# Cross-attention scores: the queries' scale moved into VectorE's pass over the scores, and the exponents' offset made by one fused pass

## The chip, the cores and the metric

The kernel runs on one core of a Trainium2 chip, as one launch. The metric is the device time of that launch in microseconds (us). The engines are TensorE (PE in the profile; PEld is its loading of weights), VectorE (DVE), ScalarE (ACT), GpSimd (POOL) and SyncE (SP), which only issues transfers.

## The reference, cut to what matters

The program is one block: a cross-attention of 512 query rows (4 x 128) to 8192 context rows, a causal self-attention, and a feed-forward network with 4-bit weights. The change lies in the cross-attention, which has 16 heads of 64 and quantises queries, keys, values and the attention weights:

```python
q = _fq_sym(q, axis=-1)          # integers -127..127, times one scale per query and head
k = _fq_sym(k, axis=-1)          # the same, one scale per key and head
v = _fq_sym(v, axis=2)
attn = jnp.einsum('bhqd,bhkd->bhqk', q, k)
attn = jax.nn.softmax(attn.astype(jnp.float32), axis=-1)
attn = _fq_unsigned(attn, axis=-1)      # rounded to multiples of (row maximum)/255
out = jnp.einsum('bhqk,bhkd->bhqd', attn, v)
```

A score is therefore (product of integers) x (scale of the key) x (scale of the query). Since the row maximum of a softmax maps to 255, the rounded weight is round(exp(score - maximum + log 255)), and the sum of the unrounded exponentials divides the result at the end.

## The kernel before, in words

The launch has stages in this order: the projection of the queries, the projection of the context to values and then to keys (up to about 1500 us), the cross-attention (about 1505 to 2144 us), the output projection and self-attention, and the feed-forward network. Only the cross-attention is touched.

Its work is cut into 64 **units** (L766), one for each head h and each block t of 128 query rows. A unit has 128 rows of scores against 8192 keys, in 8 steps of SC = 1024 keys. The loop at L981 runs over all 512 steps, and every engine's order is the order in which this loop emits instructions (a manual schedule, nothing is rearranged):

- `scores(n, g)` (L769): two matrix products (L782) put 128x1024 integer scores into PSUM (tile `sc`, two buffers). Then one custom VectorE pass, `tensor_tensor_reduce` (L789), multiplies them by the keys' scales (`sk`, spread over the partitions by GpSimd at L762), writes them to the tile `e` in SBUF, and takes the running maximum of the 1024 columns. The compiler makes two instructions of it: the pass, and a read of the accumulator into column g of `mx` (128x8).
- `maximum(n)` (L800), after the eighth step: a reduction of the eight maxima (L804) and a TENSOR_SCALAR (L806) which multiplies by minus the query's scale and adds log 255. The result `m` (128x1) is the offset of the exponents. Each of the two waits for the one before it.
- `exponentials(n, c)` (L812), twice per unit and one unit later: ScalarE forms exp(scale x e + m) over 4096 columns, rounds to int16 and sums the row (L817). The query's scale is this instruction's scale operand.
- `transposes` (L826) and `dma_transposes` (L843) turn the integers, half of them on TensorE with a copy by ScalarE (L839), half by a transfer; `values` (L874) multiplies them by the values (L881), and at the end of each head four short VectorE operations (L893 to L904) finish the result.

`sq` (L198) holds the queries' scales, 128 x 4 blocks x 16 heads. Ahead of the stage L744 makes `sqs` of it, once with the sign plus and once with minus, by two VectorE products. The tile `e` has three buffers of half a unit each, `mx` and `m` four.

The custom operation computes out = (in0 op0 in1) x scale and accumulates with op1, starting from `scalar`. Its `scale` may be a constant or a column with one value per partition.

Rows outside the stage that the prediction compares: L391 (shifts of the packed 4-bit weights, in one part by a constant, in another by the column `shifts`), L394 (a bit mask on 128x1024), L159 and L1427 (a tile times a constant plus a tile), L142 and L1167 (a layer norm's tile minus one column times another), L1534 (a 128x1 value times and plus constants), and L1541 (a tile times the column `ms` plus a tile).

Of the kernel before, what the change touches and what calls it, by code (L numbers as in the profile page):

```python
# [34 lines left out]
F32 = mybir.dt.float32  # L35
# [6 lines left out]
ALU = mybir.AluOpType  # L42
AX = mybir.AxisListType
# [3 lines left out]
P = 128  # L47
B, S, C = 4, 128, 1024
NT = B * S // P
NC = C // P  # L50
H, D = 16, 64
# [7 lines left out]
NSC = NK // SC  # L59
# [19 lines left out]
LOWEST = -3.0e38  # L79
# [7 lines left out]
def tile_perceiver(  # L87
# [26 lines left out]
    nc = tc.nc  # L114
# [83 lines left out]
    sq = qpool.tile([P, NT, H], F32, name="sq")  # L198
# [535 lines left out]
    with tc.tile_pool(name="at_e", bufs=1) as at_e, tc.tile_pool(  # L734
        name="at_s", bufs=4
    ) as small, tc.tile_pool(name="at", bufs=2) as at, tc.tile_pool(
        name="at_ps", bufs=3, space=PSUM
    ) as at_ps:
        sc_ps = sc_s.enter_context(tc.tile_pool(name="sc_ps", bufs=2, space=PSUM, side="right"))
        sv = small.tile([P, C], F32, name="sv", tag="sv", bufs=1)  # L740

        sqs = small.tile([P, 2, NT, H], F32, name="sqs", tag="sqs", bufs=1)
        for i in range(2):
            nc.vector.tensor_scalar_mul(sqs[:, i], sq, 1.0 - 2.0 * i)  # L744
        ident16 = small.tile([P, P], F16, name="ident16", tag="ident16", bufs=1)
        nc.scalar.copy(ident16, ident)
        vqs = {}
# [21 lines left out]
        def scores(n, g):  # L769

            h, t = units[n]
            if g == 0:
                mx = small.tile([P, NSC], F32, name="mx", tag="mx")
                state[n] = {"mx": mx, "e": [], "a": []}
            if g % (NSC // NEC) == 0:
                e = at_e.tile([P, EC], F32, name="e", tag="e", bufs=3)
                state[n]["e"].append(e)
            ps = sc_ps.tile([P, SC], F32, name="sc", tag="sc")

            for i in range(2):  # L780
                rows = slice(D * i, D * i + D)
                nc.tensor.matmul(  # L782
                    ps[:, ts(i, 512)],
                    lhsT=qT[rows, h, ts(t, P)],
                    rhs=kts[h, g // 2][rows, ts(g % 2, 512)],
                    start=True,
                    stop=True,
                )
            nc.vector.tensor_tensor_reduce(  # L789
                out=state[n]["e"][-1][:, ts(g % (NSC // NEC), SC)],  # L790
                in0=ps,
                in1=sks_at[h, g],
                scale=1.0,
                scalar=LOWEST,
                op0=ALU.mult,
                op1=ALU.max,
                accum_out=state[n]["mx"][:, g : g + 1],
            )

        def maximum(n):  # L800
            h, t = units[n]
            st = state[n]
            m = st["m"] = small.tile([P, 1], F32, name="m", tag="m")
            nc.vector.tensor_reduce(m, st["mx"], AX.X, ALU.max)  # L804

            nc.vector.tensor_scalar(  # L806
                m, m, sqs[:, 1, t, h : h + 1], math.log(255.0), ALU.mult, ALU.add
            )
            if t == 0:
                sums[h] = small.tile([P, NT, NEC], F32, name="sum", tag="sum")  # L810

        def exponentials(n, c):  # L812
            h, t = units[n]
            st = state[n]
            a = at.tile([P, EC], I16, name="a", tag="a", bufs=3)
            st["a"].append(a)
            nc.scalar.activation(  # L817
                a,
                st["e"][c],
                AF.Exp,  # L820
                bias=st["m"],
                scale=sqs[:, 0, t, h : h + 1],
                accum_out=sums[h][:, t, c : c + 1],
            )

# [154 lines left out]
        with tc.manual_schedule():  # L980
            for s in range(n_steps + LAG_V):  # L981
# [8 lines left out]
                if g % (NSC // NEC) == 0 and 1 <= n <= len(units):  # L990
                    exponentials(n - 1, g // (NSC // NEC))
                if n < len(units):
                    h, t = units[n]
                    scores(n, g)
                    if t == NT - 1 and h + 1 < H:

                        if g < NKC:
                            load_keys(h + 1, g)
                        spread_scales(h + 1, g)
                        if g == NSC - 1 and h + 2 < H:  # L1000
                            load_rows(h + 2)
                    if g == NSC - 1:
                        maximum(n)
# [306 lines left out]
    with tc.manual_schedule():  # L1310
# [10 lines left out]
        for h, (w, n) in enumerate(PARTS):  # L1321
# [13 lines left out]
            if h in (3, 5):  # L1335
                m = (h - 3) // 2
# [71 lines left out]
    with tc.tile_pool(name="ff_t", bufs=2) as ff_t, tc.tile_pool(  # L1408
        name="ff_a", bufs=1
# [36 lines left out]
        with tc.tile_pool(name="ff_g", bufs=2) as ff_g:  # L1446
# [13 lines left out]
            with tc.tile_pool(name="g_ps", bufs=2, space=PSUM) as g_ps, tc.tile_pool(  # L1460
                name="u_ps", bufs=2, space=PSUM
# [17 lines left out]
        with tc.tile_pool(name="ff_h", bufs=1) as ff_h, tc.tile_pool(  # L1479
            name="y_ps", bufs=1, space=PSUM  # L1480
# [135 lines left out]
```

## Time and profile before

| | us |
|---|---|
| median of 3 runs (2855.76 to 2858.63) | 2857.21 |
| the profiled execution | 2854.13 |
| its span, first to last instruction | 2852.4 |
| TensorE busy | 2652.6 |
| VectorE busy | 2421.2 |
| ScalarE busy | 1267.0 |
| GpSimd busy | 455.7 |

In the profile, a row of a group reads: line, engine, operation, output tile <- input tiles, shapes, the count, then after the bar the busy time of all in us and the mean of one in ns, and after the second bar the idle time of that engine just before these instructions, with what ended it. The page cuts the span into 40 slices, in which a digit is the busy share in tenths. A timeline row gives the start and the length in us; rows of one line in a run are merged, with their number behind the x. A table by windows gives for each stretch its length, the busy time of each engine with the number of instructions in brackets, the granted clock of TensorE, and the busy share and rate of the DMA engines. The mean granted TensorE clock of the profiled execution was 0.987.

### The profile page before, as it was taken

The numbers are of one execution on the slowest core, as the hardware profiler recorded it, in microseconds if no ns is written. First come the engines' busy times: TensorE is split into PE (matmuls) and PEld (weight loads), VectorE is DVE, ScalarE is ACT, GpSimd is POOL, SyncE is SP. The second block draws the span as 40 slices with busy tenths as digits, with TensorE's granted clock in tenths as the row PEclk, the third lists the DMA queues.
The fourth block names the chain that finished last, engine by engine and source line by source line (L and its number), as shares of the span: only waits on it lengthen the run. The fifth ranks groups of instructions, "written<-read, shape, count | busy, mean of one in ns | idle before, by whom it ended". The sixth has DMA issues, their size and how long they took to land.

```text
span 2852.4 us, 41096 instructions
## 1 busy us (share of the span) xinstructions
PE 2652.6 (93%) x15496; PEld 2059.5 (72%) x15496; DVE 2421.2 (85%) x3960; ACT 1267.0 (44%) x1404; POOL 455.7 (16%) x608
## 2 busy tenths in 40 slices
PE   8999999999999999999996777787778899999998
PEld 3788888888878888888884555555555777788886
DVE  6899999555699998888879999999997898876674
ACT  4211211112323333333217999999994244333332
POOL 0011111000012222222113332233312000000000
PEclk9999999999999999999998999999999999999999
DMA  5555565222447777777536888877875222122222
GB/s 188 170 200 201 194 212 207 104 96 95 146 106 198 192 192 186 188 186 191 130 88 144 164 167 165 154 149 161 164 145 153 76 83 67 52 96 96 94 92 96
DMA packets 450631, 412.66 MB, mean 145 GB/s; under 512 B 354872, under 2 KB 359544, under 8 KB 450432
## 3 DMA queue, kind: packets, MB, share of 16 engines
q1 hardware_dynamic: 402848, 251.70, 36.3%
q0 software_dynamic: 46528, 157.29, 17.2%
q8 instruction: 122, 2.00, 0.3%
q10 hardware_dynamic: 1056, 1.05, 0.2%
q14 instruction: 77, 0.63, 0.1%
HBM read 220.14 MB, written 104.34 MB: 114 GB/s over the span
## 4 chain that ended last, share of the span: by engine, by line
PE 70%; DVE 21%; issue 4%; POOL 2%; ACT 1%; DMA 1%; DVEq 0%; ACTq 0%
PE kv_a L342 32%; PE kv_b L342 16%; DVE e L789 14%; PE acc_a L1130 3%; PE up_a L165 3%; PE gate_a L165 3%; PE y_a L1503 3%; POOL sk L762 2%; PE q_ps L292 2%; PE acc_b L1130 1%; PE up_b L165 1%; PE gate_b L165 1%; PE y_b L1503 1%; PE a_pt L832 1%; DVE sw_l L158 1%
## 5 line engine op out<-in xcount | busy, mean ns | idle before, releaser
L342 PE MATMUL kv_b<-w_d,c_d 128*128 128x512 f32 x2048 | 806.0, 394 | 0.3 <-DVE c_d L159 0.3
L342 PE MATMUL kv_a<-w_h,c_h 128*128 128x512 f32 x2048 | 806.3, 394 | 0.0
L342 PE MATMUL kv_a<-w_l,c_l 128*128 128x512 f32 x2048 | 806.0, 394 | 0.2 <-ACT w_l L246 0.2
L789 DVE CUSTOM_DVE_ANT_0 e<-sc,sk 128x1024 f32<-128x1024 f32 x512 | 593.0, 1220 | 8.1 <-PE sc L782 7.0
L817 ACT ACTIVATE a<-e,m,sqs 128x4096 int16<-128x4096 f32 x128 | 486.9, 3804 | 24.1 <-DVE m L806 23.8
L342 PEld LDWEIGHTS kv_a<-w_l,c_l 128*128 128x128 f32 x2048 | 384.8, 188 | 89.6 <-ACT w_l L246 0.6
L342 PEld LDWEIGHTS kv_b<-w_d,c_d 128*128 128x128 f32 x2048 | 384.8, 188 | 89.5 <-DVE c_d L159 0.8
L342 PEld LDWEIGHTS kv_a<-w_h,c_h 128*128 128x128 f32 x2048 | 384.9, 188 | 88.8 <-issue 0.2
L155 ACT ACTIVATE c_h<-c_raw 128x1024 fp32r<-128x1024 f32 x128 | 135.2, 1057 | 418.9 <-PE kv_a L342 404.6
L356 DVE SCALAR_TENSOR_TENSOR f<-kv_a,bkv 128x512 f32<-128x512 f32 x256 | 175.8, 687 | 163.4 <-PE kv_a L342 162.8
L782 PE MATMUL sc<-kt,qT 64*128 64x512 bf16 x1024 | 205.5, 393 | 104.9 <-DVE mx L789 100.8
L581 ACT CAST kst<-kT 128x512 bf16<-128x512 int16 x128 | 89.4, 699 | 302.3 <-DMA kT<-ki 302.3
L832 PE MATMUL a_pt<-ident,a 128*128 128x128 f32 x1024 | 174.3, 295 | 21.1 <-ACT a L817 16.4
L357 DVE SCALAR_TENSOR_TENSOR f<-kv_b,f 128x512 f32<-128x512 f32 x256 | 176.7, 690 | 20.3 <-DVE f L356 0.9
L762 POOL PARTITION_BROADCAST sk<-sk_row x120 | 142.3, 1297 | 312.3 <-DVE mx L789 312.2
L832 PEld LDWEIGHTS a_pt<-ident,a 128*128 128x128 f32 x1024 | 111.4, 144 | 86.9 <-ACT a L817 48.9
L782 PEld LDWEIGHTS <-qT 64*128 64x128 bf16 x1024 | 75.3, 93 | 132.7 <-issue 102.7
L158 DVE TENSOR_TENSOR fw_l<-fw_raw,fw_h 128x1024 fp32r<-128x1024 f32 x64 | 78.3, 1224 | 99.4 <-ACT fw_h L155 99.3
L158 DVE TENSOR_TENSOR c_l<-c_raw,c_h 128x1024 fp32r<-128x1024 f32 x128 | 155.7, 1217 | 5.8 <-ACT c_h L155 5.6
L159 DVE SCALAR_TENSOR_TENSOR c_d<-c_l,c_raw 128x1024 fp32r<-128x1024 f32 x128 | 156.3, 1221 | 2.3
L155 ACT ACTIVATE fw_h<-fw_raw 128x1024 fp32r<-128x1024 f32 x64 | 67.8, 1060 | 175.4 <-PE y_a L1503 71.6
L548 ACT CAST vq<-vi 128x1024 f16<-128x1024 int16 x64 | 67.0, 1046 | 171.0 <-DVE vi L541 123.9
(211 smaller groups left out, 4104.9 us busy)
## 6 DMA issues: line engine op xcount, KB each, us to landing
c_raw<-in_ctxT SPq DMA_DIRECT2D x128, 512.0 KB, 3.6
v_d<-f POOLq DMA_DIRECT2D x64, 512.0 KB, 3.1
vl<-v_d POOLq DMA_DIRECT2D x64, 512.0 KB, 4.2
gu_d<-w_ffn POOLq DMA_DIRECT2D x44, 512.0 KB, 3.1
fw_raw<-gu_d SPq DMA_DIRECT2D x42, 512.0 KB, 3.2
k_d<-kst POOLq DMA_DIRECT2D x128, 128.0 KB, 3.5
vq_d<-vq POOLq DMA_DIRECT2D x32, 512.0 KB, 5.2
kt<-k_d SPq DMA_DIRECT2D x64, 256.0 KB, 3.5
```

The source lines that it names most:

```text
L155: nc.scalar.mul(hi, src, 1.0 - 0.5 / UP)
L158: nc.vector.tensor_tensor(lo, src, hi, ALU.subtract)
L159: nc.vector.scalar_tensor_tensor(df, lo, -1.0 - UP, src, ALU.mult, ALU.add)
L165: nc.tensor.matmul(ps, lhsT=lhs(i, k), rhs=rhs(i, k), start=(k == 0 and i != 1), stop=(k == NC - 1 and i != 0),)
L342: nc.tensor.matmul(ps, lhsT=tokens[s][i][:, k, :], rhs=w3[s < KT][k][i][:, ts(n, 512)], start=(k == 0 and i != 1), stop=(k == NC - 1 and i ...
L356: nc.vector.scalar_tensor_tensor(f, a, 1.0 + 1.0 / UP, bias[s < KT][n], ALU.mult, ALU.add)
L357: nc.vector.scalar_tensor_tensor(f, b, -1.0 / UP, f, ALU.mult, ALU.add)
L762: nc.gpsimd.partition_broadcast(tile_of_scales(h, g), sks_at[h][32 * c : 32 * c + 1, ts(half, SC)], channels=P)
L782: nc.tensor.matmul(ps[:, ts(i, 512)], lhsT=qT[rows, h, ts(t, P)], rhs=kts[h, g // 2][rows, ts(g % 2, 512)], start=True, stop=True,)
L789: nc.vector.tensor_tensor_reduce(out=state[n]["e"][-1][:, ts(g % (NSC // NEC), SC)], in0=ps, in1=sks_at[h, g], scale=1.0, scalar=LOWEST, o ...
L817: nc.scalar.activation(a, st["e"][c], AF.Exp, bias=st["m"], scale=sqs[:, 0, t, h : h + 1], accum_out=sums[h][:, t, c : c + 1],)
L832: nc.tensor.transpose(pt[:, i, :], a[:, at_word + P * i : at_word + P * i + P], ident)
```

## The change

The query's scale goes into the VectorE pass, whose scale operand becomes a column of `sq`. What it writes to `e` and what it takes the maximum of are then complete scores, so ScalarE's exponential has the constant 1.0 as scale. The offset log 255 - max is formed in one custom pass over the eight maxima: it adds -log 255 (a new constant tile `log255`, 128x8, written once by GpSimd), multiplies by -1, and takes the minimum. Like the large pass it is compiled to two instructions, the pass and a read of the accumulator. `sqs` and its two products go. The order of the instructions on each engine is otherwise the same.

```diff
-        sqs = small.tile([P, 2, NT, H], F32, name="sqs", tag="sqs", bufs=1)
-        for i in range(2):
-            nc.vector.tensor_scalar_mul(sqs[:, i], sq, 1.0 - 2.0 * i)
+        log255 = small.tile([P, NSC], F32, name="log255", tag="log255", bufs=1)
+        nc.gpsimd.memset(log255, -math.log(255.0))
...
                 in1=sks_at[h, g],
-                scale=1.0,
+                scale=sq[:, t, h : h + 1],
                 scalar=LOWEST,
...
             m = st["m"] = small.tile([P, 1], F32, name="m", tag="m")
-            nc.vector.tensor_reduce(m, st["mx"], AX.X, ALU.max)
-
-            nc.vector.tensor_scalar(
-                m, m, sqs[:, 1, t, h : h + 1], math.log(255.0), ALU.mult, ALU.add
+            nc.vector.tensor_tensor_reduce(
+                out=st["mx"],
+                in0=st["mx"],
+                in1=log255,
+                scale=-1.0,
+                scalar=-LOWEST,
+                op0=ALU.add,
+                op1=ALU.min,
+                accum_out=m,
             )
...
                 bias=st["m"],
-                scale=sqs[:, 0, t, h : h + 1],
+                scale=1.0,
                 accum_out=sums[h][:, t, c : c + 1],
```

## The prediction

> **What bounds the kernel now.** I read the page's slices first, to find the stage that the change lies in, then a table by windows of that stage, then its costliest groups, and at last the order of VectorE's instructions in time.
>
> The slices, 71.3 us each:
>
> ```profile
> PE   8999999999999999999996777787778899999998
> ...
> DVE  6899999555699998888879999999997898876674
> ACT  4211211112323333333217999999994244333332
> ```
>
> In the slices at 22 to 30 (1505 to 2144 us) TensorE drops to 7 or 8 tenths while VectorE and ScalarE stand at 9. This is the cross-attention, and all that the diff touches is in it. Is VectorE or ScalarE the bound there? The table by windows (length, then busy time of PE, PEld, DVE, ACT, POOL):
>
> ```profile
> 1550.00:1700.00 150.00, 117.03 (x1444) 82.24 (x1444) 147.93 (x289) 144.82 (x123) 41.30 (x47) 0.99 0.81 162
> 1700.00:1850.00 150.00, 117.51 (x1455) 82.53 (x1454) 147.91 (x289) 145.88 (x123) 46.77 (x54) 0.99 0.82 160
> ```
>
> VectorE works 148 of 150 us, ScalarE 145, TensorE 117. VectorE is the bound, with ScalarE 2% behind it. The groups say who waits for whom:
>
> ```profile
> L789 DVE CUSTOM_DVE_ANT_0 e<-sc,sk 128x1024 f32<-128x1024 f32 x512 | 593.0, 1220 | 8.1 <-PE sc L782 7.0
> L817 ACT ACTIVATE a<-e,m,sqs 128x4096 int16<-128x4096 f32 x128 | 486.9, 3804 | 24.1 <-DVE m L806 23.8
> ...
> L782 PE MATMUL sc<-kt,qT 64*128 64x512 bf16 x1024 | 205.5, 393 | 104.9 <-DVE mx L789 100.8
> ```
>
> VectorE's pass over the scores (L789) sat idle for 8.1 us in all 512 passes; ScalarE waited 23.8 us for the maximum m, TensorE 100.8 us for VectorE. So a nanosecond that is added to or taken from VectorE in this stage comes out at the end, with two limits: up to 8 us of added work can sink into VectorE's own idle time, and beyond about 24 us of saving ScalarE would take over.
>
> How VectorE spends one unit (8 passes, then the offset), from its timeline:
>
> ```profile
> 1623.90 1.22 DVE L789 CUSTOM_DVE_ANT_0 e<-sc,sk 128x1024 f32<-128x1024 f32 x1
> 1625.05 0.08 DVE L789 DVE_READ_ACCUMULATOR2_ANT mx<- 128x1 f32 x1
> 1625.17 0.16 DVE L804 TENSOR_REDUCE m<-mx 128x1 f32<-128x8 f32 x1
> 1625.36 0.21 DVE L806 TENSOR_SCALAR m<-m,sqs 128x1 f32<-128x1 f32 x1
> 1625.51 1.23 DVE L789 CUSTOM_DVE_ANT_0 e<-sc,sk 128x1024 f32<-128x1024 f32 x1
> ```
>
> A pass lasts 1.22 us, but the next one starts 1.14 to 1.15 us after it, together with the accumulator read: about 0.077 us of each instruction's length overlaps the following one. The 64 offsets each hold VectorE for 0.46 us, from 1625.05 (where the next pass could have started) to 1625.51: 0.12 until the maxima may be read, 0.19 for the reduction, 0.15 for the scaling.
>
> **Part 1: the offset by one pass.** Out go a TENSOR_REDUCE (162 ns) and a TENSOR_SCALAR (214 ns), in comes one custom pass of 128x8 and its accumulator read. No row shows a custom pass of 8 elements. Built-in rows give its length: SCALAR_TENSOR_TENSOR takes 1224 ns for 1024 elements (L159) and 689 for 512 (L1427), that is 1.045 ns per element and 154 ns fixed; for 8 elements 162 ns, just what the reduction of 8 elements takes (L804, 162 ns). The big custom pass has the same fixed part (1220 - 1024 x 1.045 = 150). With the overlap of 0.077 the next pass would start 0.085 us after it. The wait of 0.12 us for the last maximum stays, since the new pass reads the same mx. New hold: 0.12 + 0.085 = 0.205; saved 0.46 - 0.205 = 0.255 us per unit, times 64 = **-16.3 us**. If the small pass does not overlap its successor at all (0.077 more) and the read must end first (0.083 more), it is 0.095 us and -6.1. I take -16.3, because the large pass, the same kind of instruction, overlaps in every row; a dearer end of about -11 (one of the two fails) goes into the range.
>
> **Part 2: the scale as a pointer operand.** The 512 passes had an immediate 1.0 as scale; now each reads a [128,1] column of sq. No row of the trace shows a custom pass with such an operand, so I look at pairs of rows of one operation and shape, with and without it:
>
> ```profile
> L391 DVE TENSOR_SCALAR bits<-words 128x512 int32<-128x512 int32 x32 | 12.7, 419 | 0.0
> ...
> L1541 DVE SCALAR_TENSOR_TENSOR y<-y,ms,x 128x512 f32<-128x512 f32 x8 | 5.7, 748 | 0.1
> L391 DVE TENSOR_SCALAR bits<-words,shifts 128x512 int32<-128x512 int32 x12 | 5.6, 486 | 0.0
> L1427 DVE SCALAR_TENSOR_TENSOR y<-y_b,fa 128x512 f32<-128x512 f32 x8 | 5.4, 689 | 4.9 <-ACT fa L1426 4.7
> ```
>
> L391 shifts words by an immediate in 419 ns and by a column (shifts) in 486 (+67; its median is 479, +60). L1541 scales by a column (ms) in 748 ns, L1427 by an immediate in 689 (+59). A one-element TENSOR_SCALAR takes 214 ns with a column (L806) and 154 with immediates (L1534): +60. L1167 has two columns on 128x1024 and takes 813 ns where a 128x1024 TENSOR_SCALAR with none takes 689 (L394): +62 each. Is it only the length that grows, or the distance between starts too? The end of the trace has two of each back to back:
>
> ```profile
> 2840.10 1.42 DVE L1541 SCALAR_TENSOR_TENSOR y<-y,ms,x 128x512 f32<-128x512 f32 x2
> 2841.43 1.28 DVE L1427 SCALAR_TENSOR_TENSOR y<-y_b,fa 128x512 f32<-128x512 f32 x2
> ```
>
> The two with a column hold the engine from 2840.10 to 2841.43, 0.665 us each. Of the two without, the second starts 1.28 - 0.69 = 0.59 to 0.61 us after the first. The overlap of 0.07 to 0.08 stays, and the fetch of about 60 ns comes on top. So 512 x 0.060 = **+30.7 us**; with 57 ns 29.2, with 67 ns 34.3. From below: a pass is followed by an accumulator read that costs no engine time now (the next pass starts with it), and the fetch might hide in the same gap: then 0. I take 60, the value of four pairs of rows.
>
> Here a rule of the Trainium skill speaks otherwise. The page "Vector Engine (DVE) Microarchitecture Reference", section "5.2 Measured stream behaviour on trn2 (trn3 not measured)", gives built-in one- and two-source operations, and the multi-uOp programs measured, one charge of about 75 ns per instruction beside the stream, with no term for a pointer operand. The passes agree for immediates (six from 1617.04 to 1623.90 us, 1.143 apart; 1024 x 1.045 = 1070, rest 73 ns). By the rule, as an estimate, part 2 costs nothing and the whole change is -16; by the rows of the trace it is +14. The rows decide.
>
> **Part 3: the rest.** The two products that made sqs (L744, 0.20 us until L182 starts) leave VectorE ahead of the stage: -0.2. A memset of 128x8 comes to GpSimd's queue in front of a load of scale rows. In the compiled order it takes over the VectorE and TensorE wait which that load had; GpSimd is busy for 41 of 150 us in the stage, so 0. If that cover were gone it would cost one short memset. L817's scale becomes a constant: ScalarE may get shorter, not longer; 0, since VectorE ends last. No instruction of TensorE, ScalarE or SyncE moves, and each VectorE instruction keeps its place. The new pass waits where the reduction waited; behind it on VectorE are the next unit's passes. ScalarE gets m about 0.2 us after the new pass starts rather than 0.4 us, which is no use while VectorE is late.
>
> **The sum.** +30.7 - 16.3 - 0.2 = +14.2 us of VectorE. Of its 8.1 us of idle time, mostly waits of 0.2 to 0.8 us for the scores, some 2 us should vanish, as TensorE has 0.23 us more per unit to catch up: **+12.2 us**. The profiled execution took 2854.13 us (span 2852.4 and 1.7 around it): 2866.3. The median of the runs is 3.1 above it, 2857.21: **2869.4 us**. What is late next is still VectorE, and ScalarE gains idle time: a unit becomes 8 x 1.204 + 0.205 = 9.84 us against 9.61 now, ScalarE needs 9.5.
>
> **Rivals.**
> - *The fetch is hidden by the accumulator read.* For it: the read fits into the gap at no cost. Against: the gap of 0.077 us is there in L1541's pair too and the fetch is added all the same. Then -16.3 - 0.2 = -16.5, within ScalarE's 24: 2840.7. It decides at 32 ns of fetch per pass (16.5/512): below that the kernel is faster, above it slower.
> - *Half hidden*, some 30 ns: 15.4 - 16.5 = -1, 2856, no change. Nothing in the profile favours it.
> - *The small pass is dearer*, with no overlap: +30.7 - 11 or - 6.1, less 0.2: +19.5 to +24.4, 2877 to 2882. For it: no row has a short custom pass. Against: its large form has the built-in fixed part.
> - *The new pass does nothing for the offset but swaps instructions*: two for two (pass and read). Then saving 0 would need the read to cost as much as L806, where its row has 81 to 86 ns; this lies beyond the dear end.
>
> **How the numbers follow.** Fetch paid, small pass cheap: 0.72, between 29.2 - 16.5 - 6 = +6.7 and 34.3 - 16.5 = +17.8, likeliest 2869.4. Small pass dearer: 0.10, to 2882. Half hidden: 0.07. Hidden: 0.11, at 2841. A difference of 0.2% (5.7 us) is about what a measurement of this kernel can tell from no change; so slower 0.82, same 0.07, faster 0.11. The range of 2862 to 2881 us leaves out the hidden and half hidden cases and the edge of the dear one, 0.2 together.
>
> **What would show it.** In the profile after: the mean of the L789 passes of 128x1024 at 1.28 us, their starts 1.20 us apart; the 128x8 pass at 0.16 us; the distance from the last read of a unit to the next unit's pass 0.2 us in place of 0.46; ScalarE's wait for m above 23.8 us, TensorE's for mx above 100.8. I am wrong if the passes stay 1.14 us apart (the fetch is free), or if the 128x8 pass holds VectorE for 0.4 us or more.

## The result and the profile after

| us | before | after |
|---|---|---|
| median | 2857.22 (2855.76 to 2858.63, 4 runs) | 2872.36 (2870.53 to 2874.38, 4 runs) |
| the profiled execution | 2854.13 | 2871.79 |
| its span | 2852.4 | 2870.0 |
| VectorE busy | 2421.2 | 2444.1 |
| ScalarE busy | 1267.0 | 1255.7 |

The change makes the kernel 15.1 us slower: ratio 1.0049, 95% interval 1.0037 to 1.0061. Forecast were 2869.4 us (+12.2) and a range of 2862 to 2881.

The slices and the table by windows of the changed kernel (the diff moves L789 to L787, L806 to L803 and L817 to L821):

```profile
PE   8999999999999999999997787777778899999998
...
DVE  6899999555699989888879999999997898876674
ACT  4211212121323333333218999999994244333332
```

```profile
1550.00:1700.00 150.00, 116.30 (x1417) 83.41 (x1415) 148.76 (x281) 137.92 (x118) 38.73 (x44) 0.98 0.78 156
1700.00:1850.00 150.00, 117.98 (x1408) 83.89 (x1404) 147.99 (x277) 138.47 (x117) 49.87 (x55) 0.95 0.72 150
```

VectorE is as full as before, 148 to 149 of 150 us; ScalarE has gone from 145 or 146 down to 138. The bound is the same engine with more to do. The groups, with shapes kept apart:

```profile
L787 DVE CUSTOM_DVE_ANT_0 e<-sc,sk,sq 128x1024 f32<-128x1024 f32 x512 | 624.3, 1280 | 5.1 <-PE sc L780 3.7 <-ACT a L821 0.5 <-issue 0.3
L780 PE MATMUL sc<-kt,qT 64*128 64x512 bf16 x1024 | 210.8, 401 | 124.7 <-DVE mx L787 123.0 <-DVE sk_row L602 1.6
L821 ACT ACTIVATE a<-e,m 128x4096 int16<-128x4096 f32 x128 | 475.3, 3714 | 51.0 <-DVE m L803 50.7 <-DMA aT_d<-a 0.2
L803 DVE CUSTOM_DVE_ANT_0 mx<-mx,log 128x8 f32<-128x8 f32 x64 | 11.8, 184 | 2.2
```

The pass takes 1280 ns in place of 1220. ScalarE's wait for m has doubled (23.8 to 50.7 us) and TensorE's wait for VectorE has grown (100.8 to 123.0). The mean of 184 ns in the last row hides two lengths: 57 of the small passes take 167 ns and seven 0.32 us. The end of a unit in VectorE's timeline:

```profile
1624.57 1.28 DVE L787 CUSTOM_DVE_ANT_0 e<-sc,sk,sq 128x1024 f32<-128x1024 f32 x1
1625.78 0.09 DVE L787 DVE_READ_ACCUMULATOR2_ANT mx<- 128x1 f32 x1
1625.78 1.28 DVE L787 CUSTOM_DVE_ANT_0 e<-sc,sk,sq 128x1024 f32<-128x1024 f32 x1
1626.98 0.09 DVE L787 DVE_READ_ACCUMULATOR2_ANT mx<- 128x1 f32 x1
1627.11 0.17 DVE L803 CUSTOM_DVE_ANT_0 mx<-mx,log 128x8 f32<-128x8 f32 x1
1627.20 0.08 DVE L803 DVE_READ_ACCUMULATOR2_ANT m<- 128x1 f32 x1
1627.26 1.28 DVE L787 CUSTOM_DVE_ANT_0 e<-sc,sk,sq 128x1024 f32<-128x1024 f32 x1
```

Passes start 1.20 us apart (1.14 before). From the last read of the unit to the next pass, 1626.98 to 1627.26, VectorE is held for 0.28 us where it was 0.46.

Where the time is: from the start of the first pass to the start of the last, the stage took 637.5 us before (1505.05 to 2142.55) and takes 653.8 now (1504.41 to 2158.20), +16.3. Read over all 512 passes of both timelines, this is 511 x 0.0605 = +30.9 for the pass, 63 x 0.188 = -11.8 for the offset (its mean hold goes from 0.45 to 0.26 us) and 8.1 - 5.1 = -3.0 for VectorE's idle time, +16.1. After the stage nothing is changed; there the two profiled executions differ by 2 us, and those of the kernels below by up to 5.5, without a pattern that follows their edits.

### The profile page after: what moved, and what is told of

Read it like the earlier page. It is cut to its first block, busy times and chain, and to the rows that moved or that the text cites. A ratio compares the mean times of both kernels' runs of the same rounds, so it can differ in the third digit from the quotient of the medians.

```text
span 2870.0 us, 41095 instructions
## 1 busy us (share of the span) xinstructions
PE 2667.9 (93%) x15496; PEld 2074.2 (72%) x15496; DVE 2444.1 (85%) x3958; ACT 1255.7 (44%) x1404; POOL 460.2 (16%) x609
## 4 chain that ended last, share of the span: by engine, by line
PE 71%; DVE 22%; issue 5%; ACT 2%; DMA 1%; DVEq 0%; SPq 0%; ACTq 0%
PE kv_a L342 33%; PE kv_b L342 16%; DVE e L787 16%; PE acc_a L1134 3%; PE y_a L1507 3%; PE gate_a L165 3%; PE up_a L165 3%; PE up_b L165 1%; PE gate_b L165 1%; PE y_b L1507 1%; PE acc_b L1134 1%; PE q_ps L292 1%; PE a_pt L836 1%; DVE sw_l L158 1%; PE sc L780 1%
## 5 line engine op out<-in xcount | busy, mean ns | idle before, releaser
L787 DVE CUSTOM_DVE_ANT_0 e<-sc,sk,sq 128x1024 f32<-128x1024 f32 x512 | 624.3, 1280 | 5.1 <-PE sc L780 3.7
L821 ACT ACTIVATE a<-e,m 128x4096 int16<-128x4096 f32 x128 | 475.3, 3714 | 51.0 <-DVE m L803 50.7
L780 PE MATMUL sc<-kt,qT 64*128 64x512 bf16 x1024 | 210.8, 401 | 124.7 <-DVE mx L787 123.0
L760 POOL PARTITION_BROADCAST sk<-sk_row x120 | 144.7, 1299 | 318.7 <-DVE mx L787 318.6
L780 PEld LDWEIGHTS <-qT 64*128 64x128 bf16 x1024 | 84.6, 93 | 153.7 <-issue 124.3
```

The lines of the kernel that those rows point to most:

```text
L760: nc.gpsimd.partition_broadcast(tile_of_scales(h, g), sks_at[h][32 * c : 32 * c + 1, ts(half, SC)], channels=P)
L780: nc.tensor.matmul(ps[:, ts(i, 512)], lhsT=qT[rows, h, ts(t, P)], rhs=kts[h, g // 2][rows, ts(g % 2, 512)], start=True, stop=True,)
L787: nc.vector.tensor_tensor_reduce(out=state[n]["e"][-1][:, ts(g % (NSC // NEC), SC)], in0=ps, in1=sks_at[h, g], scale=sq[:, t, h : h + 1], ...
L821: nc.scalar.activation(a, st["e"][c], AF.Exp, bias=st["m"], scale=1.0, accum_out=sums[h][:, t, c : c + 1],)
```

## The experiments

The theory: each pass pays for fetching its column, and the fused offset gives back a part. ("Fetch" is only a name here for the time that a column costs; the runs measure that time and not how it arises.) The rivals: the fetch is free and the loss comes from elsewhere in the change; the fused pass saves nothing. Beside experiments 1 to 4 the kernel before took 2858.25 us (median of 9 runs), beside 5 to 8 it took 2856.61; ratios and differences are to these.

**1. A column of ones, nothing else (in the kernel before).**

```diff
+        ones = small.tile([P, 2], F32, name="ones", tag="ones", bufs=1)
+        nc.gpsimd.memset(ones[:, 0:1], 1.0)
+        nc.gpsimd.memset(ones[:, 1:2], LOWEST)
...
-                scale=1.0,
+                scale=ones[:, 0:1],
```

The second column is filled but not used; the next experiment uses it.

> The kernel before, with one change: the scale of the 512 passes is a column that holds 1.0 in place of the constant 1.0, so nothing that is computed changes. Theory (a column operand costs a fetch of 60 ns on VectorE at each pass): the 128x1024 pass takes 1.28 us, starts lie 1.204 us apart, the offset still holds VectorE for 0.45 us per unit; 512 x 0.0605 = +31.0, some 3 us of it sink into VectorE's idle time: 2885 us. Rival (the fetch is free, and the changed kernel is slower because of something else that it does, the constant scale on ScalarE or the new offset pass): 2857 us.

Measured: 2892.96 us beside 2858.25, ratio 1.0122 (1.0108 to 1.0136), +34.7. The kernel computes what it computed, with one operand in another form:

```profile
L792 DVE CUSTOM_DVE_ANT_0 e<-sc,sk,ones 128x1024 f32<-128x1024 f32 x512 | 625.0, 1280 | 10.9 <-PE sc L785 10.1 <-ACT a L820 0.6
```

The pass is at 1280 ns, as in the changed kernel, and the starts of two passes lie 1.204 us apart. The rival that the fetch is free falls. The loss is 8 us above the theory's number: VectorE's idle time has not shrunk by 3 us but grown from 8.1 to 10.9, and all the growth is waiting for scores. More on this below.

**2. Two columns.** As above, and the starting value of the maximum is a column too.

```diff
-                scale=1.0,
-                scalar=LOWEST,
+                scale=ones[:, 0:1],
+                scalar=ones[:, 1:2],
```

> As with the column of ones, and the starting value of the maximum is a column too (it holds -3e38): two column operands per pass. Theory (each column is fetched for itself): pass 1.34 us, starts 1.264 us apart, 512 x 0.121 = +62 us, less 3: 2916 us. Rival (both come with one fetch): as with one column, 2885 us.

Measured: 2926.21 us, ratio 1.0239 (1.0223 to 1.0254), +68.0.

```profile
L792 DVE CUSTOM_DVE_ANT_0 e<-sc,sk,ones 128x1024 f32<-128x1024 f32 x512 | 657.4, 1341 | 13.3 <-PE sc L785 12.4 <-ACT a L820 0.4
```

1220, 1280, 1341 ns for no, one and two columns: each is paid for itself, 60 and 61 ns. Again the idle time grows (13.3).

**3. The scale alone.** The changed kernel, with the offset by a reduction and a second operation, with constants.

```diff
-            nc.vector.tensor_tensor_reduce(
...
-                accum_out=m,
-            )
+            nc.vector.tensor_reduce(m, st["mx"], AX.X, ALU.max)
+            nc.vector.tensor_scalar(m, m, -1.0, math.log(255.0), ALU.mult, ALU.add)
```

> The changed kernel with the offset made as before by a reduction and a second operation, here with two constants (x -1, + log 255). Theory: passes at 1.28 us as in the changed kernel; the hold per unit 0.12 + 0.20 + 0.08 = 0.40 us against 0.258 with the fused pass, 64 x 0.14 = +9: 2881 us; against the column of ones it is 64 x 0.06 = 4 us faster, since L806's counterpart has no column. Rival (the fused pass saves nothing): 2872 us.

Measured: 2893.47 us, ratio 1.0129 (1.0115 to 1.0143), 21.1 us slower than the changed kernel and level with the column of ones. Two parts of what was expected failed. The hold is 0.44 us and not 0.40, so that the shorter second operation (153 ns against 214) brought almost nothing: in the timelines the next pass starts 0.12 us after the start of the second operation in most units, where it was 0.13 before, and not 0.08 (only the first unit has 0.07). And VectorE waits longer for scores:

```profile
L787 DVE CUSTOM_DVE_ANT_0 e<-sc,sk,sq 128x1024 f32<-128x1024 f32 x512 | 625.8, 1280 | 12.4 <-PE sc L780 11.7 <-ACT a L814 0.5
```

The fused pass thus saves 63 x 0.18 = 11.5 us of hold here, and the waiting is 12.4 - 5.1 = 7.3 us shorter with it: 18.8 of the 21.1. The rival (it saves nothing) falls. Why the waiting shrinks with the fused pass was not found.

**4. The offset alone.** The kernel before, with only the fused pass. Since the scores are now without the query's scale s, the pass forms (max - log 255 / s) x (-s).

```diff
+        lsq = small.tile([P, NT, H], F32, name="lsq", tag="lsq", bufs=1)
+        nc.vector.reciprocal(lsq, sq)
+        nc.vector.tensor_scalar_mul(lsq, lsq, -math.log(255.0))
...
-            nc.vector.tensor_reduce(m, st["mx"], AX.X, ALU.max)
-            nc.vector.tensor_scalar(
-                m, m, sqs[:, 1, t, h : h + 1], math.log(255.0), ALU.mult, ALU.add
-            )
+            nc.vector.tensor_tensor_reduce(
+                out=st["mx"],
+                in0=st["mx"],
+                in1=lsq[:, t, h : h + 1].to_broadcast([P, NSC]),
+                scale=sqs[:, 1, t, h : h + 1],
+                scalar=-LOWEST,
+                op0=ALU.add,
+                op1=ALU.min,
+                accum_out=m,
+            )
```

> The other half alone: the passes keep their constant scale and ScalarE keeps the query's scale; only the offset is made by one custom pass over the eight maxima, as (max - log 255 / s) x (-s), with a column of s as scale and a column of -log 255 / s (made once ahead of the stage by two short VectorE operations) as second input. Theory: the pass has the 166 ns seen in the changed kernel plus a fetch of 60; hold per unit 0.12 + 0.09 + 0.06 + 0.03 = 0.30 us against 0.454 before: 64 x 0.154 = -9.9, the preparation +0.5: 2848 us. Rival (the custom pass on eight elements is no cheaper than the two operations that it replaces): 2857 us or above.

Measured: 2847.80 us, ratio 0.9967 (0.9954 to 0.9979), -10.4 us. This half of the change is a gain by itself. The two halves do not add up: the scale alone costs 35.2 us and the offset alone gains 10.4, which makes +24.8, but together they cost 15.1. A part of this is that the changed kernel waits less for scores (3.7 us) than the scale alone (11.7). And ScalarE is now close behind inside a head: 101 of the 127 distances between the starts of its exponentials are the 4.74 or 4.75 us at which it works without a pause, where it was 62 before.

The pass takes 227 ns as a rule (60 more than without a column, so a short custom pass pays the same), but in seven units 0.74 to 0.75 us. The first of them and a pass that kept its length, each with GpSimd's broadcast in which it starts:

```profile
1583.76 1.30 POOL L765 PARTITION_BROADCAST sk<-sk_row  x1
1584.19 0.75 DVE L807 CUSTOM_DVE_ANT_0 mx<-mx,lsq,sqs 128x8 f32<-128x8 f32 x1
...
1624.60 1.30 POOL L765 PARTITION_BROADCAST sk<-sk_row  x1
1625.60 0.23 DVE L807 CUSTOM_DVE_ANT_0 mx<-mx,lsq,sqs 128x8 f32<-128x8 f32 x1
```

In the last unit of a head (all heads but the last) the pass always starts during a broadcast; what differs is how far into it. The seven long passes start 0.43 to 0.45 us after the start of their broadcast, the others 1.00 us (one 0.92 us, and it takes 0.27), and the long ones all end at the same point, 1.18 or 1.19 us after that start. The changed kernel has seven passes of 0.32 us in place of 0.17. They start 0.86 us into a broadcast and end at the same 1.18 or 1.19, so 0.32 and 0.75 differ by where the pass starts, not by its column. The broadcasts keep their mean length (1297 ns in the kernel before and here, 1299 in the changed one): it is VectorE's pass that is held.

**5. The offset by the fused pass in three of four units.** The edit, against the kernel of experiment 4:

```diff
+            if t == NT - 1:
+                nc.vector.tensor_reduce(m, st["mx"], AX.X, ALU.max)
+                nc.vector.tensor_scalar(
+                    m, m, sqs[:, 1, t, h : h + 1], math.log(255.0), ALU.mult, ALU.add
+                )
+            else:
                 nc.vector.tensor_tensor_reduce(
```

> The offset alone by the fused pass, but only in three of four units: in the last unit of each head, in which GpSimd spreads the next head's scales, the offset is made as in the kernel before. Theory (the seven fused passes of 0.74 us in the offset-alone kernel are held by GpSimd's broadcasts, and a reduction and a TENSOR_SCALAR, with one SBUF tensor each, are not): no long pass remains; 7 x (0.79 - 0.454) = -2.4 us, the other 9 such units +0.19 each: 2847 us, equal to the offset alone within 2 us. Rival (the long passes come from the unit's place, whatever the operation): a reduction or TENSOR_SCALAR of about 0.7 us shows in its place.

Measured: 2845.89 us, ratio 0.9960 (0.9947 to 0.9972). Per unit as expected: no long operation is left, neither the fused pass (227) nor the two in its place (162 and 215):

```profile
L813 DVE CUSTOM_DVE_ANT_0 mx<-mx,lsq,sqs 128x8 f32<-128x8 f32 x48 | 10.9, 227 | 1.7
...
L809 DVE TENSOR_SCALAR m<-m,sqs 128x1 f32<-128x1 f32 x16 | 3.4, 215 | 0.6
...
L808 DVE TENSOR_REDUCE m<-mx 128x1 f32<-128x8 f32 x16 | 2.6, 162 | 0.6
```

Seven of these reductions start 0.44 or 0.45 us into a broadcast, where the long passes had started, and keep their 0.16 us. So it is not the place that makes the long passes, but this form of operation in this place. It has two SBUF tensors, the reduction and the TENSOR_SCALAR have one, and so has the large pass, which reads its scores from PSUM and runs at 1.22 us under the broadcasts. (The Trainium skill, page "VectorE: DVE Perf Modes", section "Two Vector instructions with no wait between them", says in a comment that a second SBUF tensor comes through a read interface shared with GpSimd. That fits, but no run here varied the number of SBUF tensors alone.) In time the two versions cannot be told apart, but both beat the kernel before and the changed one.

**6. A part of the offset on ScalarE.**

```diff
+        log255 = small.tile([P, 1], F32, name="log255", tag="log255", bufs=1)
+        nc.gpsimd.memset(log255, math.log(255.0))
...
             nc.vector.tensor_reduce(m, st["mx"], AX.X, ALU.max)
-            nc.vector.tensor_scalar(
-                m, m, sqs[:, 1, t, h : h + 1], math.log(255.0), ALU.mult, ALU.add
-            )
+            nc.scalar.activation(
+                m, m, AF.Identity, bias=log255, scale=sqs[:, 1, t, h : h + 1]
+            )
```

> The kernel before, with the second half of the offset moved: VectorE only reduces the eight maxima, and ScalarE multiplies by minus the query's scale and adds log 255 (one activation on 128x1, ahead of its exponentials). This takes the TENSOR_SCALAR off VectorE (hold per unit 0.23 us in place of 0.454, which alone would give 64 x 0.22 = -14) and loads ScalarE, which needs 9.5 us per unit, with about 0.2 us of its own, 0.09 for its column and 0.1 to 0.2 until the exponential may read the result: 9.85 us per unit, as much as VectorE's 9.87 before (9.61 and a quarter of the 1.03 us at the end of each head). Theory (ScalarE is a close second bound, as the prediction had it): 2857 us, within 4 us, with VectorE now waiting for ScalarE. Rival (ScalarE has room): 2843 us.

Measured: 2874.32 us, ratio 1.0061 (1.0045 to 1.0078). VectorE's hold fell to 0.25 us, about as expected, and the kernel is 17.7 us slower than before. The rival falls, and the theory's 2857 us is missed too: it had the right engine and too small a price. From ScalarE's timeline, and from the table of waits (engine and line <- what it waited for: us in all, times, the longest):

```profile
1617.58 3.80 ACT L819 ACTIVATE a<-e,m,sqs 128x4096 int16<-128x4096 f32 x1
...
1627.07 0.41 ACT L808 ACTIVATE m<-m,log,sqs 128x1 f32<-128x1 f32 x1
1627.51 3.80 ACT L819 ACTIVATE a<-e,m,sqs 128x4096 int16<-128x4096 f32 x1
...
PE a_pt L834 <- ACT a L819: 60.1, 85, 2.3
```

The small activation holds ScalarE for 0.44 us (1627.07 to 1627.51), so a unit takes it 9.93 us (1617.58 to 1627.51) where VectorE's mean was 9.87. VectorE's passes now stand idle for 32.7 us, 23.8 of it for scores. TensorE is late with them because it stands at its transposes: there it waits 60.1 us for ScalarE's exponentials, 16.4 in the kernel before. The chain of work that ended last agrees: between 1510 and 2130 us ScalarE's exponentials hold 55% of it and VectorE's pass 13%, where it was 1% and 62% in the kernel before. So ScalarE has become the bound. Why the kernel loses 17.7 us, and not the little that 9.93 against 9.87 would make, was not taken apart.

**7. and 8. TensorE kept busy.** In experiments 1 to 3 VectorE waits longer for scores although it asks for them less often. What does TensorE do then? The kernel before has an instance at 1892 us. In the table by windows, the last three columns are TensorE's granted clock, the DMA share and its rate:

```profile
1885.10:1888.50 3.40, 1.59 (x22) 1.05 (x22) 3.33 (x9) 3.40 (x5) 0.00 (x0) 1.00 0.37 69
1888.50:1891.90 3.40, 3.40 (x28) 2.27 (x26) 2.85 (x6) 3.40 (x1) 0.00 (x0) 0.53 0.84 159
```

In one stretch of 3.4 us TensorE is busy for 1.59 us only (it waits 1.35 us for the end of a head, `xo`). In the next it runs at about half clock, is busy all the time, and VectorE waits 0.71 us for scores at its end. The Trainium skill, page "TensorE: Matmul & The Clock Gate", section "Part 1: The HAM clock gate (the "warmup" mystery)", describes a free-running window of about 3.4 us, and half rate after an idle one; here a stretch with 1.59 us of work was already followed by half rate. Over the stage the granted clock of the profiled executions is 0.97 before, 0.95 in the changed kernel, 0.94, 0.93 and 0.91 in experiments 1, 3 and 2. Two kernels give TensorE needless work at every step, the first half of a score product made once more and overwritten:

```diff
+            nc.tensor.matmul(
+                ps[:, 0:256],
+                lhsT=qT[0:D, h, ts(t, P)],
+                rhs=kts[h, g // 2][0:D, ts(2 * (g % 2), 256)],
+                start=True,
+                stop=True,
+            )
             for i in range(2):
```

One is the column of ones with this addition, the other the fused offset in three of four units.

> The column of ones again, and TensorE gets needless work: at each of the 512 steps the first half (256 columns) of the first score product is made once more and overwritten by the real one. Theory (the part of the loss that exceeds the fetch comes from TensorE: with a slower VectorE it idles more, its granted clock falls to one half for single windows of 3.4 us, and VectorE then waits for scores): with TensorE busier the dips go, the waits of L792's pass for scores fall from 10.1 us to 4 or less, and the time falls by some 6 us against the column of ones, to 2887 us. Rival (TensorE is late because it has too much work): more work for it makes these waits longer, 2893 us or above.

> The previous kernel (fused offset in three of four units) with the needless quarter of the score products that keeps TensorE busy. Theory (dips of the granted clock cost this stage some us in every version): the passes' waits for scores fall from 6 us to 2 or 3, so 2843 us. Rival (TensorE becomes the bound, at 117 of 150 us plus about 0.11 us per step): 2850 us or above.

Measured: with the column of ones 2895.69 us, ratio 1.0137 (1.0123 to 1.0151), waits for scores 14.6 us in place of 10.1, granted clock of the stage 0.94 as without the addition: the dips did not go, the expected gain did not come, and the rival's number is the one that was met, so that too much work for TensorE is not ruled out as the cause there. With the fused offset 2846.13 us, ratio 0.9963 (0.9949 to 0.9976): in the profiled executions the clock of the stage is 0.98 in place of 0.96 and the waits for scores are 5.5 us in place of 7.8, but the time is that without the addition, neither the theory's 2843 nor the rival's 2850. Even this rise is not safely the edit's: over the whole launch the profiled execution without the addition had the lowest clock of its five runs (0.984, the others 0.986 or 0.987), and with the addition all five have 0.987 or 0.988. Nor do waits and clock go together in every version: the changed kernel has 0.95 and waits only 3.7 us for scores, the kernel before 0.97 and 7.0. So it is open why VectorE waits longer in experiments 1 to 3. The dips delay it where one can be watched, as at 1892 us; that they are the cause of the longer waits is not shown.

## Why the prediction was right

- **VectorE is the bound.** Right: 148 to 149 of 150 us before and after, and ScalarE's and TensorE's waits for it grew as stated.
- **The fetch, 60 ns in each pass, +30.7.** Right in length (1220 to 1280) and in distance (0.0605 us, +30.9), taken from built-in operations of other shapes. The rule that was weighed against it, one charge per instruction whatever its operands, would have had +0 here; experiments 1 and 2 settle it for the rows. The rival of a hidden fetch is out: the distance between passes grew by as much as their length, so the accumulator read hides nothing of it.
- **The fused pass, -16.3.** Right in direction, too large: -11.8. Its length was estimated as 162 ns and is 167. The step that failed is "the next pass would start 0.085 us after it". This holds in the first unit, where the read and the next pass both start at 1514.26, 0.09 us after the pass at 1514.17; in most others a further 0.03 to 0.06 us follow the read. The same floor shows in the other kernels: from the start of the last short operation to the start of the next pass it is 0.11 to 0.16 us, also where that operation is as short as 153 ns (experiment 3), and where it lasts 227 ns (experiment 4) the pass follows its read without a gap. In the compiled order these later passes wait for two engines (TensorE's scores and ScalarE's release of `e`), the first for TensorE alone; that this is the cause is argued from the order, not tried. Seven passes of 0.32 us add 1 us. The mean hold is 0.26 us, where 0.205 was forecast.
- **Idle time, some 2 us to vanish.** 3.0 vanished. That was luck: the reason given (TensorE has time to catch up) does not hold in experiments 1 to 3, where VectorE is just as slow or slower and the idle time grew by 3 to 5 us. The prediction had no term for TensorE's clock, which fell in all of them.
- **ScalarE as the next bound.** Its nearness was right, and experiment 6 ran into it. Its own gain from the constant scale (3804 to 3714 ns, 90 ns per exponential) was not needed, as stated.
- **The sum.** +30.9 - 11.8 - 3.0 = +16.1 against +14.2 - 2 = +12.2; the medians say +15.1. The difference of the two sums is, in the main, the 4.5 us by which the fused pass was overrated, less 1 us of idle time.

## What to carry to other kernels

In these traces a per-partition column in place of a constant costs a VectorE instruction some 60 ns each, in operations of 1 element per partition (154 to 214 ns) as in a custom pass of 1024 (1220 to 1280). Put such a column on the operation that runs least often, and price it from any pair of rows in the trace that differ in this alone. Of a change with two parts on one engine, price and try each for itself: here one half is a gain of 10 us and the other a loss of 35 (together 15, since the waits for scores differ too), and the first half alone, with the scale left where it ran 64 and 128 times, is the better kernel.

## What the runs showed of the hardware that was not expected

- A constant in place of a column makes ScalarE's exponential on 128x4096 90 ns shorter (3804 to 3714), and a 128x1 activation with two columns takes 0.41 us, twice what the square root of a 128x1 column takes (203 ns).
- A custom VectorE pass of eight elements with two SBUF tensors was held when it started 0.43 to 0.86 us into a GpSimd broadcast of 1.30 us: it ended 1.18 or 1.19 us after the broadcast's start and so took 0.32 us in place of 0.17, or 0.75 in place of 0.23. A reduction with one SBUF tensor that started at the same point did not grow.
- With a slower VectorE TensorE's granted clock fell (0.97 of the stage, 0.94 with one column, 0.91 with two). In the same kernels VectorE's idle time grew (8.1, 10.9 and 13.3 us); that the one causes the other is not shown.
